# Attention of a vision transformer layer: weighted values and their sums as four streams of 256 queries, four tiles of exponentials, and matrix pieces run whole or in quarters

## The chip, the cores and the metric

One core of one Trainium2 chip runs the whole kernel as one program. The metric is the device time of one execution in microseconds (us); "the median" is the median over several executions. TensorE is the matrix engine (PE in the profile; its weight loads are listed apart as PEld), VectorE is DVE, ScalarE is ACT, GpSimd is POOL, and SyncE (SP) issues the transfers.

## The reference

Sixteen images of 512x512 are cut into 1,024 patches each and embedded into 256 channels. One transformer layer follows: attention with 8 heads of 32 channels, where every key is first sent through a sum of 256 sines and 256 cosines, and then a network with a shared branch and four experts of which two are weighed in. Cut to what matters here:

```python
h = patches(x) @ W.T + b
qkv = layernorm(h) @ w_qkv
q, k, v = to_heads(split(qkv))
k = sum(a[f] * sin(f * k) + b[f] * cos(f * k) for f in 1..256)
attn = softmax(q @ k.T / sqrt(32))
h = h + (attn @ v) @ w_out + b_out
h = h + shared(layernorm(h)) + sum(top2 weights * experts(layernorm(h)))
```

The softmax is not shifted by its maximum here: the kernel computes exponentials, the weighted sum of the values, and the sum of the exponentials, and divides at the end. All of it is fp32.

## The kernel before

The plain path (`plain_path`) builds the whole instruction stream for the 16 images in Python, with an order that a planner decides while building. The planner keeps an estimated clock for each engine.

*The two kinds of work.* Work with a **fixed order** makes up rounds. There are 128 attention steps (16 images, 4 pairs of heads, 2 halves of 512 queries) and 512 groups of key transforms, so each round has four groups and one attention step, which belongs to the groups of two rounds earlier:

- a group (`load_waves`, `turn_waves`, `sine`, `mix`, `times_fast`): two tiles w and one tile f are turned on POOL, go through the sine on ScalarE (`sine`, L972, after a table load at the first of a round), are mixed on TensorE in eight tiles of 64x32 (`mix`, L996, written kan) and multiplied on VectorE (`times_fast`, L1010, "prod"). `add_up` (L1029, written red) sums products over two groups.
- an attention step: eight tiles of scores (`score`, L1094, written sT, two matmuls of 512 columns), their exponentials (`exponential`, L1109, written es), eight weighings (`weigh`, L1126, written av), and `normalize` (L1152 to L1171) on VectorE. `ATTENTION` gives the order on TensorE: s is a score with its exponential, w a weighing, r a sum of products: "ssssrwwsswwsswwww". So four scores come first, then weighings and scores in pairs, and after the eighth score four more weighings.

On ScalarE each round is: one table load for the sine, twelve sines, one table load for the exponential (L1240), eight exponentials.

**Pieces** are the rest, generators in four chains: `tokens` (tok, the patch embedding, 6 matmuls of 256 columns), `keys` (k), `queries` (q), `values` (v), `project` (proj), `gates`, and `networks` (s1p, s2p, e1p, e2p, wb, e3p). Where a generator says `yield GO` it wants TensorE next. `run` decides each time whether the fixed head or a piece goes: a piece may go when it is ready clearly before the fixed work (by `IDLE`, or, when the fixed head has the same tiling as the array now, by two `SWITCH`), or when it is due. `retile` counts a change of tiling at `SWITCH`, 0.18 us, in the planner's clock.

*Tilings.* Most pieces, scores and transposes use the whole array of 128x128. Weighings, sums of products, gates and the experts' second layer use four column tiles of 128x32 side by side (`TILINGS`), and the mixing uses 64x32.

*Buffers that matter.* Two big PSUM buffers are shared in turn by kan and sT, so a score waits until the product or the exponential two places earlier has read its buffer (`big_deps`). The exponentials have three tiles (`esp`): an exponential waits for the weighing three places earlier. One PSUM bank holds the accumulator of the weighings (`avp`): the next step's first weighing waits for `normalize`. Two `side` banks serve the pieces.

*Weighing before.* The 512 columns of the accumulator are 512 queries. Its 128 rows are, in four blocks of 32: the values of head 0, the sums of head 0, the sums of head 1, the values of head 1. The tile v has 96 columns for each pair: values, ones, values. So four matmuls of 512 columns run side by side, two of them against ones:

```python
for i in range(4):
    nc.tensor.matmul(
        out=acc[0][ts(i, HD), :],
        lhsT=v[:, kc, p % NPAIR, ds(HD * (i - i // 2), HD)],
        rhs=es[:, ts(i // 2, 512)], ...
```

`normalize` takes reciprocals of the whole accumulator in two halves of 256 columns, multiplies 32x512 for each head, and adds up a check over 128x512.

Of the kernel before, what the change touches and what calls it, by code (L numbers as in the profile page):

```python
# [18 lines left out]
P = 128  # L19
E = 256  # L20
NPAIR = 4
HD = 32
# [25 lines left out]
NW = 8  # L48
GS = 4
NW5 = 4 * (NE + 1)  # L50
PE, ACT, DVE, POOL, SP = "pe", "act", "dve", "pool", "sp"
GO = PE, None
# [6 lines left out]
TILINGS = {"mix": (64, 32), "av": (128, 32), "red": (128, 32)}  # L59
ATTENTION = "ssssrwwsswwsswwww"  # L60

@with_exitstack
def plain_path(ctx: ExitStack, tc: tile.TileContext, a: dict, out: bass.AP, verdict: bass.AP):
# [29 lines left out]
    esp = pool("esp", 3)  # L93
# [107 lines left out]
    v = const.tile([P, NT, NPAIR, 96], FP, tag="v", name="v")  # L201
    nc.gpsimd.memset(v[:, :, :, 32:64], 1.0)
# [43 lines left out]

    def together(at, queue):
# [18 lines left out]
    def matmul(out, lhsT, rhs, start, stop):  # L266
        now["stream"] += max(rhs.shape[-1], P)
        nc.tensor.matmul(out=out, lhsT=lhsT, rhs=rhs, start=start, stop=stop)  # L268
# [23 lines left out]
    def step(c):  # L292
# [6 lines left out]
        on = need[0] if isinstance(need, tuple) and need[0] in clock else None  # L299
        if on:  # L300
# [40 lines left out]
    def wanting(engine):  # L341

        for c, ch in enumerate(chains):
# [3 lines left out]
            if len(need) > 2 and now["table"] != need[2]:  # L347
                continue
# [53 lines left out]

    def run():

        while True:
# [8 lines left out]
                or (at < fixed[0] - 2 * SWITCH if follows else at < then - IDLE)  # L414
                or (not follows and chains[c]["due"] > 0 and at <= then)
# [64 lines left out]
    def tokens(b, half):  # L480
# [5 lines left out]
        for t in range(4):  # L486
            j = 4 * half + t
            yield "x", b, j
            yield GO
# [28 lines left out]
    def keys(b, rows, blks=(0, 1)):  # L518
# [7 lines left out]
        for blk in blks:  # L526
            yield "hnT", b, blk
            yield GO
# [44 lines left out]
    def queries(b, rows):  # L573
# [7 lines left out]
        for blk in range(2):  # L581
            yield GO
# [14 lines left out]
    def values(b):  # L597
# [5 lines left out]
        for t0 in range(0, NT, 2):  # L603
            yield GO
# [12 lines left out]
            for s in range(2):  # L617
                nc.scalar.copy(
                    v[:, ds(t0, 2), 0 : NPAIR - 1, ds(64 * s, HD)],
# [5 lines left out]
    def last_values(b):  # L625
# [3 lines left out]
        for s in range(2):  # L629
            nc.gpsimd.tensor_copy(  # L630
                v[:, :, NPAIR - 1, ds(64 * s, HD)], images[b]["last"][:, :, s, :]
# [61 lines left out]
    def project(b, half):  # L693
# [3 lines left out]
        for pr in range(2):  # L697
            yield GO
# [19 lines left out]
    def gates(b, half, late=False):  # L718
# [9 lines left out]
        yield GO  # L728
# [11 lines left out]
        now["piece"] = TILINGS["red"]  # L740
# [18 lines left out]
    def networks(b, half, late=False):  # L759
# [25 lines left out]
        def first_of_expert(e):  # L785
            yield GO
# [6 lines left out]
        def second_of_experts(u, e1):  # L793
            yield GO
            ps = side_tile("e2p")
            now["piece"] = TILINGS["av"]
# [25 lines left out]
        for m in range(2):  # L822
            yield GO
# [4 lines left out]
        yield GO  # L828
# [276 lines left out]
    def exponential(att, kc):  # L1105
# [6 lines left out]
        old = att * NT + kc - 3  # L1112
# [4 lines left out]
    def weigh(att, kc):  # L1117
# [3 lines left out]
        def action():  # L1121
# [3 lines left out]
            for i in range(4):  # L1125
                nc.tensor.matmul(  # L1126
                    out=acc[0][ts(i, HD), :],
                    lhsT=v[:, kc, p % NPAIR, ds(HD * (i - i // 2), HD)],
                    rhs=es[:, ts(i // 2, 512)],
                    start=(kc == 0),  # L1130
                    stop=(kc == NT - 1),
                )
# [9 lines left out]
    def normalize(att):  # L1142
# [4 lines left out]
        def reciprocal(half):  # L1147
            def action():
                if half == 0:
                    rc[0] = kup.tile([P, 512], FP, tag="rc", name="rc")  # L1150
# [24 lines left out]
        for half in range(2):  # L1175
            reciprocal(half)
# [826 lines left out]
```

## Time and profile before

| | |
|---|---|
| median of 3 executions | 4131.01 us (4130.44 to 4134.47) |
| the profiled execution's own time | 4124.1 us |
| its span on the core | 4122.6 us, mean granted TensorE clock 0.994 |
| share of 16 transfer engines' time | 80.2% for the main queue |
| weighing av, TensorE | 8192 matmul records, 956.9 us busy, mean 596 ns |
| score sT, TensorE | 2048 records, 691.5 us, mean 449 ns |
| mixing kan, TensorE | 8192 records, 635.0 us, mean 600 ns |
| exponential es, ScalarE | 1024, 1035.8 us, mean 1023 ns |
| sine w and f, ScalarE | 1024 and 512, 1020.7 and 513.6 us, mean 1048 ns |
| reciprocal rc, VectorE | 256 of 128x256, 431.8 us, mean 1727 ns |
| division aT, VectorE | 256 of 32x512, 176.1 us, mean 688 ns |
| check rc, VectorE | 128 of 128x512, 87.1 us, mean 680 ns |
| one image (eight rounds) in the middle | 248 us, from a last score to that of eight steps later |

An fp32 matmul has two records (two passes over its columns); the scores are in a format with one pass. Matmuls overlap, so a record's mean length is longer than what it adds to the time: what counts is the distance from one start to the next. Busy times are unions of the records and hold some waiting. The record of an engine that waits shows the idle time in front of it and who ended it.

### The profile page before, as it was taken

The page shows a single profiled execution, that of the slowest core. Times are in us where ns is not written, and L with a number is a line of the kernel's source. Part 1 is how long each engine was busy: PE and PEld are TensorE (multiplying, and loading weights), DVE is VectorE, ACT ScalarE, POOL GpSimd, SP SyncE. Part 2 cuts the span into 40 slices and gives each one's busy share as a digit, 9 for nine tenths or more (in the row PEclk, how much of TensorE's full clock was granted, in tenths as well). Part 3 has the DMA queues.
Part 4 walks back from the last instruction along what each step waited for, and adds up shares of the span by engine and source line. Part 5 has one row for each costly group of instructions (what it writes and reads, how often), then busy time and mean ns, then how long its engine had stood idle before and what let it go on. Part 6 is the DMA issues. An engine that isn't in the chain of part 4 may idle for free.

```text
span 4122.6 us, 76263 instructions
## 1 busy us (share of the span) xinstructions
PE 3972.3 (96%) x27105; PEld 1756.1 (43%) x27105; DVE 2818.9 (68%) x4172; ACT 3283.9 (80%) x3939; POOL 3195.2 (78%) x2328
## 2 busy tenths in 40 slices
PE   7889999999999999999999999999999999999998
PEld 4324344444444444444444444444444444443334
DVE  4666767777667776767767667776767767668652
ACT  2688888888888878888788888878888788888873
POOL 3988878787787887878787787887878788787750
PEclk9999999999999999999999999999999999999999
DMA  7998878878878888888888878888888878878850
GB/s 219 262 246 220 245 206 225 247 220 226 236 213 244 233 233 220 225 241 225 244 221 225 235 215 241 234 232 220 225 241 223 247 217 225 236 204 235 211 144 17
DMA packets 587512, 914.82 MB, mean 222 GB/s; under 512 B 58828, under 2 KB 177524, under 8 KB 587124
## 3 DMA queue, kind: packets, MB, share of 16 engines
q1 hardware_dynamic: 580880, 906.98, 80.2%
q8 instruction: 218, 3.57, 0.4%
q10 hardware_dynamic: 6244, 2.88, 0.3%
q14 instruction: 170, 1.39, 0.1%
HBM read 758.64 MB, written 150.99 MB: 221 GB/s over the span
## 4 chain that ended last, share of the span: by engine, by line
PE 60%; ACT 16%; DMA 8%; DVE 6%; issue 5%; SPq 3%; POOL 1%; ACTq 0%; DVEq 0%; POOLq 0%
PE av L1126 14%; PE sT L1094 10%; ACT w L972 7%; PE kan L996 6%; PE tok L268 5%; PE red L1029 5%; PE e1p L268 4%; DMA w<-ud 4%; ACT f L972 3%; PE proj L268 3%; SPq L926 2%; PE k L268 2%; PE q L268 2%; DVE f L1010 2%; PE s1p L268 2%
## 5 line engine op out<-in xcount | busy, mean ns | idle before, releaser
L962 POOL TENSOR_TENSOR w<-w,lane 128x1024 int32<-128x1024 int32 x1024 | 1924.9, 1895 | 535.4 <-DMA w<-ud 300.0
L1109 ACT ACTIVATE es<-sT 128x1024 f32<-128x1024 f32 x1024 | 1035.8, 1023 | 531.0 <-PE av L1126 303.3
L962 POOL TENSOR_TENSOR f<-f,lane 128x1024 int32<-128x1024 int32 x512 | 970.1, 1895 | 145.1 <-DVE f L947 127.6
L972 ACT ACTIVATE w<-w 128x1024 f32<-128x1024 int32 x1024 | 1020.7, 1048 | 36.9 <-POOL w L962 25.0
L1126 PE MATMUL av<-es,v 128*32 128x512 f32 x8192 | 956.9, 596 | 2.2 <-DVE rc L1171 2.2
L1152 DVE RECIPROCAL rc<-av 128x256 f32<-128x256 f32 x256 | 431.8, 1727 | 544.1 <-PE av L1126 544.1
L1094 PE MATMUL sT<-q,k 128*128 128x512 f32 x2048 | 691.5, 449 | 44.9 <-DVE f L1010 27.0
L1010 DVE TENSOR_TENSOR f<-kan,f 128x1024 f32<-128x1024 f32 x512 | 604.3, 1218 | 142.2 <-ACT f L972 112.6
L996 PE MATMUL kan<-w,coef 64*32 64x512 f32 x8192 | 635.0, 600 | 47.4 <-ACT w L972 46.4
L947 DVE STREAM_SHUFFLE f<-src 128x1024 int32<-128x1024 int32 x512 | 674.6, 1360 | 0.5
L1094 PEld LDWEIGHTS sT<-q,k 128*128 128x128 f32 x2048 | 348.5, 189 | 422.1 <-issue 178.5
L972 ACT ACTIVATE f<-f 128x1024 f32<-128x1024 int32 x512 | 513.6, 1048 | 2.8 <-POOL f L962 2.8
L1126 PEld LDWEIGHTS av<-es,v 128*32 128x32 f32 x8192 | 239.7, 109 | 552.9 <-issue 493.0
L268 PE MATMUL tok<-wt,x 128*128 128x256 f32 x1536 | 363.3, 388 | 17.0 <-DMA x<-in_xT 13.1
L268 PEld LDWEIGHTS tok<-wt,x 128*128 128x128 f32 x1536 | 291.3, 193 | 98.8 <-issue 37.1
L996 PEld LDWEIGHTS kan<-w,coef 64*32 64x32 f32 x8192 | 135.0, 105 | 420.4 <-ACT w L972 266.9
L1029 PE MATMUL red<-f,pack 128*32 128x512 f32 x2048 | 273.6, 604 | 1.5 <-DVE f L1010 1.3
L268 PE MATMUL e1p<-hT,w1e 128*128 128x512 f32 x480 | 234.2, 610 | 0.8 <-ACT s L826 0.4
L972 ACT ACT_TABLE_LOAD x128 | 164.2, 1283 | 22.2 <-DMA w<-ud 19.9
L1159 DVE TENSOR_TENSOR aT<-av,rc 32x512 f32<-32x512 f32 x256 | 176.1, 688 | 6.7
L467 ACT ACTIVATE hn<-h,less,rstd 128x256 f32<-128x256 f32 x256 | 144.1, 593 | 37.8 <-POOL less L459 37.8
L1240 ACT ACT_TABLE_LOAD x128 | 164.2, 1283 | 2.3
(129 smaller groups left out, 3726.4 us busy)
## 6 DMA issues: line engine op xcount, KB each, us to landing
w<-ud SPq DMA_DIRECT2D x2048, 256.0 KB
q<-qd SPq DMA_DIRECT2D x512, 128.0 KB
k<-kd SPq DMA_DIRECT2D x128, 512.0 KB
x<-in_xT SPq DMA_DIRECT2D x128, 384.0 KB
ud<-u SPq DMA_DIRECT2D x64, 512.0 KB
ud<-ui SPq DMA_DIRECT2D x64, 512.0 KB
src<-ud SPq DMA_DIRECT2D x512, 64.0 KB
qd<-qhi SPq DMA_DIRECT2D x64, 256.0 KB
```

The costliest lines, as they stand in the source:

```text
L268: nc.tensor.matmul(out=out, lhsT=lhsT, rhs=rhs, start=start, stop=stop)
L947: nc.vector.stream_shuffle(w, sources[g // 8].rearrange("p r n -> p (r n)"), [4 * (g % 8) + i // 8 for i in range(32)],)
L962: nc.gpsimd.tensor_tensor(w, w, f.to_broadcast([P, N]), ALU.mult)
L972: nc.scalar.activation(x, w, AF.Sin, scale=TURN * 2.0**-32)
L996: nc.tensor.matmul(out=ps[ds(64 * j + 32 * blk, 32), ts(r, 512)], lhsT=coef[ts(r, 64)].rearrange("p e f j -> p (e f j)"), rhs=w[ts(r, 64), ...
L1010: nc.vector.tensor_mul(w, kan.pop(g), w)
L1029: nc.tensor.matmul(out=rows_of_pair[p][ts(2 * i + r, 32), :], lhsT=pack[:, ds(PACK0 - 16 * (k % 2) - 2 * (k // 2), 32)], rhs=prod[:, ts(r, ...
L1094: nc.tensor.matmul(out=ps[:, ts(s, 512)], lhsT=k4[:, 2 * s + kc // 4, ts(kc % 4, P)], rhs=q4[:, s, :], start=True, stop=True,)
L1109: nc.scalar.activation(es, scores.pop(kc), AF.Exp, scale=SCALE)
L1126: nc.tensor.matmul(out=acc[0][ts(i, HD), :], lhsT=v[:, kc, p % NPAIR, ds(HD * (i - i // 2), HD)], rhs=es[:, ts(i // 2, 512)], start=(kc == 0),
L1152: nc.vector.reciprocal(rc[0][:, part], acc[0][:, part])
L1159: nc.vector.tensor_mul(aT[ds(64 * (i % 2) + HD * s, HD), i // 2, ts(qb, 512)], acc[0][ds(96 * s, HD), :], rc[0][ds(HD + HD * s, HD), :],)
```

## The change

- The weighing becomes eight matmuls of 256 columns. The four column tiles are now head 0 and head 1 of the first 256 queries, then head 0 and head 1 of the second 256. The first four matmuls put the weighted values into columns 0 to 255, the other four the sums into columns 256 to 511 of the same rows, against a tile of ones of its own (`ones32`). The ones leave v, which has 64 columns for each pair.
- `normalize` takes one reciprocal of 128x256, divides 64 rows by 256 columns twice, and its check covers 128x256.
- The exponentials have four tiles in place of three (`NES`), so each waits for the weighing four places earlier.
- `GO` now says "whole". Pieces that say `ANY` are whole matmuls when the array is whole, and quarters when it is in column tiles: each matmul is then issued as four of 32 output rows. After kan, `tiling_of` looks at the next three fixed entries. Of the pieces tok, k, q, v, proj, s1p, e1p and s2p are of this kind. The gates and the experts' second layer, which were in column tiles before, say "columns"; transposes, wb and e3p stay whole.
- In `run`, the stricter rule against a piece that would break a tiling is applied only when the piece would have another tiling (`apart`). `ATTENTION` and the due times are as before.

```diff
-GO = PE, None
+NES = 4
+GO = PE, None, "whole"
+ANY = PE, None, "either"
+COLUMNS = (128, 32)
...
-    esp = pool("esp", 3)
+    esp = pool("esp", NES)
...
-    v = const.tile([P, NT, NPAIR, 96], FP, tag="v", name="v")
-    nc.gpsimd.memset(v[:, :, :, 32:64], 1.0)
+    v = const.tile([P, NT, NPAIR, 2 * HD], FP, tag="v", name="v")
+    ones32 = const.tile([P, HD], FP, tag="ones32", name="ones32")
+    nc.gpsimd.memset(ones32, 1.0)
...
+    def tiling_of(kind):
+        if kind == "columns":
+            return COLUMNS
+        if kind == "whole":
+            return None
+        if now["tiling"] in (None, COLUMNS):
+            return now["tiling"]
+        ahead = [TILINGS.get(key[0]) for _, _, key, _ in queues[PE]["fixed"][:3]]
+        return COLUMNS if COLUMNS in ahead and None not in ahead[: ahead.index(COLUMNS)] else None
...
     def matmul(out, lhsT, rhs, start, stop):
         now["stream"] += max(rhs.shape[-1], P)
-        nc.tensor.matmul(out=out, lhsT=lhsT, rhs=rhs, start=start, stop=stop)
+        if now["piece"] != COLUMNS:
+            nc.tensor.matmul(out=out, lhsT=lhsT, rhs=rhs, start=start, stop=stop)
+            return
+        for i in range(4):
+            nc.tensor.matmul(
+                out=out[ts(i, 32)], lhsT=lhsT[:, ts(i, 32)], rhs=rhs, start=start, stop=stop
+            )
...
+    def apart(c):
+        return tiling_of(chains[c]["need"][2]) != now["tiling"]
...
-                or (at < fixed[0] - 2 * SWITCH if follows else at < then - IDLE)
-                or (not follows and chains[c]["due"] > 0 and at <= then)
+                or (at < fixed[0] - 2 * SWITCH if follows and apart(c) else at < then - IDLE)
+                or (not (follows and apart(c)) and chains[c]["due"] > 0 and at <= then)
...
-            yield GO
+            yield ANY
             ps = side_tile("tok")[:, 0:E]
...
-        old = att * NT + kc - 3
+        old = att * NT + kc - NES
         if old >= 0:
             deps.append(("av", *divmod(old, NT)))
...
-            for i in range(4):
-                nc.tensor.matmul(
-                    out=acc[0][ts(i, HD), :],
-                    lhsT=v[:, kc, p % NPAIR, ds(HD * (i - i // 2), HD)],
-                    rhs=es[:, ts(i // 2, 512)],
-                    start=(kc == 0),
-                    stop=(kc == NT - 1),
-                )
+            for half in range(2):
+                for i in range(4):
+                    nc.tensor.matmul(
+                        out=acc[0][ts(i, HD), ts(half, 256)],
+                        lhsT=ones32 if half else v[:, kc, p % NPAIR, ts(i % 2, HD)],
+                        rhs=es[:, ds(512 * (i % 2) + 256 * (i // 2), 256)],
+                        start=(kc == 0 and half == 0),
+                        stop=(kc == NT - 1),
+                        skip_group_check=True,
+                    )
...
-                nc.vector.reciprocal(rc[0][:, part], acc[0][:, part])
+            nc.vector.reciprocal(rc[0], acc[0][:, 256:512])
...
-                    aT[ds(64 * (i % 2) + HD * s, HD), i // 2, ts(qb, 512)],
-                    acc[0][ds(96 * s, HD), :],
-                    rc[0][ds(HD + HD * s, HD), :],
-                )
+                    aT[ds(64 * (i % 2), 2 * HD), i // 2, ds(512 * qb + 256 * half, 256)],
+                    acc[0][rows, 0:256],
+                    rc[0][rows, :],
+                )
```

## The prediction

> **What bounds the kernel now.** I read the page's engine shares first, then the chain of waits in one stretch of the middle, then the waits of all engines, then the timeline of two engines at the end of an attention step.
>
> ```profile
> PE 3972.3 (96%) x27105; PEld 1756.1 (43%) x27105; DVE 2818.9 (68%) x4172; ACT 3283.9 (80%) x3939; POOL 3195.2 (78%) x2328
> ```
>
> TensorE is busy 96% of the span; no other engine is above 80%. A busy TensorE is not yet a streaming one, so the next view, the chain of waits (start, length, what), tells what each piece costs after each neighbour.
>
> ```profile
> 2020.51 1.88 PE kan L996 x32
> 2022.38 1.00 PE red L1029 x8
> 2023.38 1.91 PE e1p L268 x4
> 2025.30 0.93 PE sT L1094 x4
> 2026.22 1.72 PE q L268 x4
> 2027.94 0.93 PE sT L1094 x4
> 2028.87 0.99 PE red L1029 x8
> 2029.87 1.72 PE av L1126 x16
> 2031.58 1.92 PE s2p L268 x4
> ...
> 2034.42 1.85 PE av L1126 x16
> ```
>
> The same work has two prices. A two-chunk piece of 512 columns is 1.72 us after whole-array work (q) and 1.91 to 1.92 after 32-column work (e1p after red, s2p after av). A pair of weighings is 1.72 after red, which has their tiling, and 1.85 after a score. So a change of tiling costs about 0.195 us into the whole array and 0.13 into column tiles. By the same subtraction over the middle of the trace: 0.165 from whole to the 64x32 tiles of kan (1.88 against 1.72), 0.195 from kan to whole, 0.135 from kan to columns (0.99 for a red of 0.858), 0.15 to 0.16 from columns to kan. Nothing else separates the pieces: TensorE is bound by streaming plus changes of tiling, and by some waits:
>
> ```profile
> ACT es L1109 <- PE av L1126: 303.3, 348, 4.0
> ACT es L1109 <- PE sT L1094: 225.1, 267, 8.9
> PE kan L996 <- ACT w L972: 46.4, 59, 4.8
> PE sT L1094 <- DVE f L1010: 27.0, 61, 1.0
> ```
>
> TensorE waits for ScalarE's sines, and for big PSUM buffers that the products and exponentials free. ScalarE waits much longer for TensorE: 303 us of that is an exponential that wants one of three tiles back from a weighing.
>
> ```profile
> 2037.63 1.50 PE L1094 MATMUL sT<-q,k 128*128 128x512 f32 x4
> 2038.81 1.02 ACT L1109 ACTIVATE es<-sT 128x1024 f32<-128x1024 f32 x1
> 2039.06 3.64 PE L1126 MATMUL av<-es,v 128*32 128x512 f32 x32
> 2040.25 1.02 ACT L1109 ACTIVATE es<-sT 128x1024 f32<-128x1024 f32 x1 [0.42 <-PE av L1126]
> 2041.29 1.28 ACT L972 ACT_TABLE_LOAD   x1
> 2042.59 1.06 ACT L972 ACTIVATE w<-w 128x1024 f32<-128x1024 int32 x1
> ```
>
> These are the last two scores of a step (7th and 8th), their exponentials, the four weighings, and the start of the next round's sines. The eighth exponential starts 0.42 us after the seventh is done, because it waits for the fifth weighing. From here to the next step's exponentials ScalarE has table load, twelve sines, table load; in this stretch ScalarE and not TensorE is short of time.
>
> [...] The trace has a pass of 512 columns fp32 at 0.429 us (1.72 for four), and one of 256 columns at 0.2158 (12 tok passes in 2.59). [...]
>
> **The change part by part.** The sum is against the profiled execution (4124.1 us, span 4122.6); the median of the runs, 4131.0, lies 6.9 above it and gets the same difference.
>
> 1. *Weighing as 8 matmuls of 256 columns in place of 4 of 512.* Four column tiles run together, so a step was 2 x 0.429 = 0.858 and becomes 4 x 0.2158 = 0.863: 1,024 steps x 0.005 = +5 us. Twice as many matmuls and weight loads: a weight load of 32 columns takes 110 ns (row of L1126), less than a pass of 0.216, and gate, which streams only 128 columns through four column tiles, does its 16 records in 0.44 us behind a weighing, at 0.109 per pass. So weight loads hide.
>
> 2. *Pieces in quarters.* A whole piece of 512 columns and four quarters side by side stream equally long (1.72 for q, 1.72 for two weighings). What goes is changes of tiling. I counted them in the two orders of TensorE's instructions:
>
>    Whole to columns 474 before and 409 after; columns to whole 558 and 461; whole to kan 279 and 132; kan to whole 195 and 80; kan to columns 118 and 245; columns to kan 34 and 193.
>
>    At the prices above (0.155 for the last) this is 275.7 us before and 243.5 after. With part 1, streaming and changes of tiling together come to 3824.6 us before and 3797.7 after: **-26.9 us**. 1,176 matmuls of tok, k, q, v, proj, s1p, s2p, e1p become quarters.
>
> 3. *Where the pieces now lie.* Because a quarter piece no longer breaks the tiling, the rule lets it between two weighings. TensorE's work from the fourth to the eighth score of a step grows from 7.51 to 8.19 us, and its work from the eighth score to the fourth of the next step falls from 20.89 to 19.99 (means over 121 middle rounds). In that second stretch ScalarE needs 18.77 us from the start of the eighth exponential to the end of the next step's second, which the fourth score waits for (18.86 after), at the pitches of the trace: sine 0.946, exponential 0.915, table load 1.29, hidden layers 0.57, normalizing 0.49. So the pieces move out of the stretch in which ScalarE is late, 0.9 us per round.
>
> 4. *Four tiles of exponentials.* With three, the eighth exponential waits for the fifth weighing; with four for the fourth, which is done before the eighth score. From the end of the eighth score's streaming to the start of its exponential the trace has 1.62 us on the mean (median 1.29). By the same instructions at the same prices it comes to 1.67 before; after, the seventh exponential or the eighth score sets it, 0.73. ScalarE starts its stretch 0.94 us sooner: about what part 3 takes.
>
>    I summed parts 3 and 4 round by round. For each landmark (kan of the four groups, each score of the next step, its weighings) I took ScalarE's or VectorE's work up to it less TensorE's work up to it, both from the eighth score, and of these the largest if above nothing. Before: 124.9 us in 121 rounds. The trace, as time between eighth scores less streaming and changes of tiling, has 174.1, with a correlation of 0.94 over the rounds and 1.20 x sum + 0.20 us per round as the fit. After: 107.4, by the fit 153.2: **-20.9 us**. With three tiles in the new order the sum would be 197.1, by the fit 260.5: +86. So this is the small difference of two large terms and the least certain one.
>
> 5. *Normalizing.* Two reciprocals (1.727 each), two divisions (0.688) and the check (0.680) become one reciprocal, two divisions of 64x256 and a check of 128x256. The nearest row for these is h<-tok, 128x256, 0.406. Per step 5.5 us becomes 3.0, some 320 us of VectorE in all. In the middle it is hidden: the next weighing comes 20 us later. Two steps at the end are bare: the timeline has a weighing at 4039.41 that waits 2.17 for the check, and projections behind the last division. **-4 us.** Less VectorE work ahead of the products could give a few us more, or nothing; I take nothing.
>
> 6. *Rest.* A smaller memset of v at the start, gates' and experts' second layer with their tiling named: nothing, same instructions.
>
> Sum: -26.9 - 20.9 - 4 = -51.8, so 4072 for the profiled execution and **4079** for the median.
>
> **The rivals.**
>
> *Rival 1, slower: ScalarE's start isn't earlier.* Place: the eighth exponential. If it still starts 1.3 us or more behind its score (the seventh being late, or pieces before the eighth score), part 4 falls away and part 3 stays: +86 - 26.9 - 4 = +55, 4186. Between -51.8 at a mean start of 0.73 us and +55 at 1.67, in proportion, it turns slower by over 0.2% from 1.26 us on. For it: 303 us of such waits are there, and the pieces do move into the weighings. Against: in the lines above the seventh exponential was done 0.42 before.
>
> *Rival 2, slower: TensorE can't take the instructions so fast.* 27,105 matmul records become about 42,350, in runs of 54 ns each where it streams 256 columns (22,300 of them). The trace of before shows that rate only in bursts (kan: 32 records in 1.72 us); over 64 records its best is 78 ns. [...]
>
> *Rival 3, no change: the waits eat the gain.* For it: the middle of a small difference is soft, and the rounds of after are less alike. If the waits grow by what the changes of tiling save, 4131 - 27 + 27 - 4 = 4127. Against: the fit holds with a correlation of 0.94.
>
> *Rival 4, faster still.* Products come sooner on a freer VectorE, and half of the 153 us of waits goes too: 4131 - 27 - (174 - 77) - 4 = 4003. For it: 27 us of waits of scores for products. Against: those products wait for sines themselves.
>
> **How the numbers follow.** Forecast (4050 to 4115): 0.62. Rival 4 and what lies below 4050: 0.08. Rival 3, within 0.2% (8 us, about what a measurement of this kernel tells from no change): 0.12. Rival 1: 0.12. Rival 2: 0.06. Faster 0.70, same 0.12, slower 0.18. The range takes in the no-change case and half of rival 4's room: 4045 to 4142 leaves out rivals 1 and 2 and the lowest values.
>
> **What would show it.** In the chain: a quarter piece after av or kan at 1.72 and 1.85 in place of 1.91; a pair of weighings at 1.73 after red; gaps of 0.2158 per pass. In the timeline: the eighth exponential right behind the seventh. Among the waits: es <- av far below 303 us; kan <- w and sT <- es no larger than now. VectorE's busy time near 2,500 us. Wrong would be: av steps above 0.87 us (rival 2), kan and sT waits that grow (rival 1).

## The result, and the profile after

| | before | after |
|---|---|---|
| median of 4 executions | 4130.73 us | 4085.28 us (4081.02 to 4097.31) |
| ratio, 95% interval | 1 | 0.9893 (0.9871 to 0.9915) |
| the profiled execution's own time | 4124.1 us | 4081.02 us |
| its span | 4122.6 us | 4079.5 us |
| matmul records | 27,105 | 42,353 |

The changed kernel is faster by 45 us, 1.1%, in the medians, and by 43.1 us in the spans of the two profiled executions. The forecast was 4079 us. A single execution can lie several us to either side: 23 of the kernel before ran from 4125.4 us (mean granted clock 0.994) to 4142.5 (0.990). The page's engine shares of the changed kernel come first:

```profile
PE 3925.2 (96%) x42353; PEld 1889.6 (46%) x42353; DVE 2538.8 (62%) x4044; ACT 3252.8 (80%) x3939; POOL 3196.3 (78%) x2328
```

TensorE is again busy for 96% of the span, now with 56% more records. VectorE gave up 280 us of work. The chain of waits in the middle of the changed kernel's trace (start, length, what):

```profile
2002.16 1.02 PE kan L1020 x16
2003.18 1.85 PE e1p L287 x16
2005.03 1.02 PE kan L1020 x16
2006.05 1.00 PE red L1053 x8
2007.05 1.32 PE sT L1118 x4
...
2010.54 0.99 PE red L1053 x8
2011.53 1.73 PE av L1151 x32
2013.26 0.44 PE wb L284
2013.69 0.92 PE sT L1118 x4
2014.62 1.86 PE av L1151 x32
...
2028.78 1.88 PE kan L1020 x32
2030.66 1.86 PE v L287 x32
2032.52 2.77 PE kan L1020 x32
2035.29 1.00 PE red L1053 x8
2036.29 1.73 PE v L287 x32
```

Here kan is the mixing, red a sum of products, sT a score and av a weighing; L287 is a piece in quarters, L284 a whole one. A quarter piece of v behind red, which has its tiling, is 1.73 us, where a whole e1p in that place was 1.91. Behind kan it is 1.85 or 1.86. A pair of weighings is now 32 records, and still 1.73 behind red and 1.86 behind a score. So in these lines streaming cost nothing more, and a quarter piece meets the array as a weighing does. The kan at 2032.52 shows what is left: 2.77 us for the 32 records that take 1.88 at 2028.78 in the same trace, so some 0.9 us of it is a wait.

The waits of the changed kernel (engine, line, for whom; total, times, longest):

```profile
DVE rc L1175 <- PE av L1151: 611.0, 114, 9.8
ACT es L1133 <- PE sT L1118: 479.7, 310, 8.6
...
PE kan L1020 <- ACT w L996: 44.6, 54, 3.7
PE sT L1118 <- ACT es L1133: 21.3, 47, 1.2
PE sT L1118 <- DVE f L1034: 16.3, 28, 2.7
...
PE sT L1118 <- DMA k<-kd: 8.9, 6, 2.7
```

One line of the kernel before belongs beside them:

```profile
PE sT L1094 <- ACT es L1109: 12.0, 35, 0.8
```

The 303.3 us in which an exponential waited for a weighing are gone; the exponentials now wait for their scores alone. But TensorE's own waits hardly moved: kan for sines went from 46.4 to 44.6 us, scores for products from 27.0 to 16.3, and scores for exponentials rose from 12.0 to 21.3, which the prediction had named as a sign of being wrong. In six places a score now waits for the transfer of its keys, 8.9 us in all; the kernel before has no such wait, and the same order in experiments 1, 2 and 4 has 1.3 to 1.7 us of it. The wait that vanished was ScalarE's, and the sums below show how little of it reached the time.

The timeline of TensorE and ScalarE over the end of an attention step of the changed kernel:

```profile
2047.43 1.21 PE L1118 MATMUL sT<-q,k 128*128 128x512 f32 x4
2048.27 1.94 ACT L1133 ACTIVATE es<-sT 128x1024 f32<-128x1024 f32 x2 [1.06 <-PE sT L1118]
...
2049.02 0.61 PE L1151 MATMUL av<-es,ones 128*32 128x256 f32 x8
...
2049.89 0.61 PE L1151 MATMUL av<-es,ones 128*32 128x256 f32 x8
...
2050.22 1.28 ACT L996 ACT_TABLE_LOAD   x1
...
2050.75 0.61 PE L1151 MATMUL av<-es,ones 128*32 128x256 f32 x8
```

The four matmuls are the seventh and eighth scores. Their exponentials are one stretch of 1.94 us with nothing between them, and the table load follows 0.01 us behind. Before, 0.42 us lay between the two.

I split the difference of 43.1 us in the spans by the prediction's own terms. "List" is streaming plus changes of tiling at the prediction's prices, over the whole program. "Waits" is the time between eighth scores in 121 middle rounds less the list's part of it; it is what is left over, and not idle time alone. "Lateness" is the prediction's sum over these rounds, computed from each kernel's order of instructions and not from its time. The last column but one is the mean distance in the middle rounds from the end of the eighth score's streaming to its exponential.

| | list | waits | lateness | eighth exponential behind | span |
|---|---|---|---|---|---|
| before | 3824.6 us | 174.1 us | 124.9 us | 1.61 us | 4122.6 us |
| after | 3797.7 us | 171.7 us | 107.4 us | 0.76 us | 4079.5 us |

The list gives -26.9, the waits -2.4, the stretch ahead of the middle rounds -4.3 beyond the list's part and the stretch behind them -9.3 (from 115.6 us in all to 106.3, with 88 us of list in both): -42.9 together. So in these two traces the gain is the changes of tiling, the end and the start. The waits, from which the prediction had expected 20.9 us, gave next to nothing. TensorE's idle time by the pages, span less busy time, didn't fall either: 150.3 us before and 154.3 after. Each of these figures is from one execution, so a difference of a few us among the waits, between these two or any two programs below, is not to be relied on.

### The profile page after: what moved, and what is told of

The parts are those of the page before. It is cut to its first block, busy times and chain, and to the rows that moved or that the text cites. A ratio compares the mean times of both kernels' runs of the same rounds, so it can differ in the third digit from the quotient of the medians.

```text
span 4079.5 us, 106618 instructions
## 1 busy us (share of the span) xinstructions
PE 3925.2 (96%) x42353; PEld 1889.6 (46%) x42353; DVE 2538.8 (62%) x4044; ACT 3252.8 (80%) x3939; POOL 3196.3 (78%) x2328
## 4 chain that ended last, share of the span: by engine, by line
PE 59%; ACT 16%; DMA 11%; DVE 5%; issue 4%; SPq 2%; POOL 2%; ACTq 0%; DVEq 0%; POOLq 0%
PE av L1151 14%; PE sT L1118 10%; ACT w L996 7%; PE kan L1020 6%; DMA w<-ud 6%; PE e3p L284 4%; PE red L1053 4%; PE tok L284 4%; ACT f L996 3%; PE e1p L287 2%; DVE f L1034 2%; ACT es L1133 2%; PE tok L287 2%; SPq L950 2%; PE e1p L284 2%
## 5 line engine op out<-in xcount | busy, mean ns | idle before, releaser
L1133 ACT ACTIVATE es<-sT 128x1024 f32<-128x1024 f32 x1024 | 1006.0, 1022 | 481.1 <-PE sT L1118 479.7
L1118 PE MATMUL sT<-q,k 128*128 128x512 f32 x2048 | 668.8, 439 | 52.1 <-ACT es L1133 21.3
L1020 PE MATMUL kan<-w,coef 64*32 64x512 f32 x8192 | 612.7, 600 | 44.9 <-ACT w L996 44.6
L1151 PE MATMUL av<-es,v 128*32 128x256 f32 x8192 | 637.7, 383 | 1.2 <-ACT es L1133 1.2
L1151 PE MATMUL av<-es,ones 128*32 128x256 f32 x8192 | 631.0, 380 | 0.0
L1175 DVE RECIPROCAL rc<-av 128x256 f32<-128x256 f32 x128 | 224.9, 1757 | 611.0 <-PE av L1151 611.0
L1151 PEld LDWEIGHTS av<-es,ones 128*32 128x32 f32 x8192 | 266.7, 110 | 177.2 <-issue 2.1
L284 PE MATMUL tok<-wt,x 128*128 128x256 f32 x792 | 185.0, 385 | 13.3 <-DMA w1s<-in_sW 13.1
L287 PE MATMUL tok<-wt,x 128*32 128x256 f32 x2976 | 172.2, 379 | 3.2 <-DVE ui L579 3.2
L284 PEld LDWEIGHTS tok<-wt,x 128*128 128x128 f32 x792 | 152.0, 193 | 38.1 <-issue 13.5
```

Source lines behind the costliest of these rows:

```text
L287: nc.tensor.matmul(out=out[ts(i, 32)], lhsT=lhsT[:, ts(i, 32)], rhs=rhs, start=start, stop=stop)
L1020: nc.tensor.matmul(out=ps[ds(64 * j + 32 * blk, 32), ts(r, 512)], lhsT=coef[ts(r, 64)].rearrange("p e f j -> p (e f j)"), rhs=w[ts(r, 64), ...
L1118: nc.tensor.matmul(out=ps[:, ts(s, 512)], lhsT=k4[:, 2 * s + kc // 4, ts(kc % 4, P)], rhs=q4[:, s, :], start=True, stop=True,)
L1133: nc.scalar.activation(es, scores.pop(kc), AF.Exp, scale=SCALE)
L1151: nc.tensor.matmul(out=acc[0][ts(i, HD), ts(half, 256)], lhsT=ones32 if half else v[:, kc, p % NPAIR, ts(i % 2, HD)], rhs=es[:, ds(512 * ( ...
L1175: nc.vector.reciprocal(rc[0], acc[0][:, 256:512])
```

## The experiments

Each has its median and its ratio to the kernel before with a 95% interval, both from runs on one chip. That kernel's median was between 4130.5 and 4138.1 from one group of runs to another, so ratios are what is compared across groups. Where a difference of medians across groups is given, the one by ratios stands beside it, in us of a kernel before of 4131; the spans and the waits are those of one profiled execution each.

**1. Whole pieces in the changed kernel's order.** On the changed kernel; the order and every wait stay, and the pieces are whole matmuls wherever they stand.

```diff
-        if now["piece"] != COLUMNS:
+        if True:
```

> The changed kernel with its order of instructions untouched, but every piece issued as whole matmuls. Theory A (changes of tiling cost what the chain shows): changes of tiling rise from 1520 to 1743 in the plain path, and streaming plus changes from 3797.7 to 3844.6 us, +47; the waits stay or fall a little, since TensorE has more to do where ScalarE is late (round sums 107 to 99). So 30 to 47 us above the changed kernel, about 4125. Rival B (quarters gain nothing, the gain lies in the fourth tile and VectorE): within 10 us of the changed kernel.

4129.5 us, ratio 0.9989 (0.9982 to 0.9996): slower than the changed kernel by 44 us in the medians and by 40 in the ratios. The list says +47 (3844.6 against 3797.7, with 1743 changes of tiling in place of 1520). The waits come out the same, 171.7. So in this order quarters are worth, within some 10 us, what counting changes of tiling says. Note where it ends, though: the new order without quarters is as slow as the old one.

**2. Three tiles of exponentials in the changed kernel's order.**

```diff
-    esp = pool("esp", NES)
+    esp = pool("esp", 3)
```

> The changed kernel with its order untouched and three tiles of exponentials in place of four. Theory A: the eighth exponential waits for the fifth weighing again, its start behind the eighth score goes from 0.76 to about 1.7 us on the mean, and the round sums from 107 to 197 us; +86 to +110, about 4180 to 4195, slower than the kernel before. Rival C (ScalarE has slack there, the fourth tile only moves idle time): within 15 us of the changed kernel.

4198.31 us, ratio 1.0155 (1.0135 to 1.0176), 113 us slower than the changed kernel in the medians and 108 in the ratios, a little above the range expected. The list is the same, the waits are 287.2 in place of 171.7, the eighth exponential stands 1.77 us behind its score. The waits of this kernel:

```profile
ACT es L1133 <- PE av L1151: 417.2, 360, 4.6
ACT es L1133 <- PE sT L1118: 237.6, 264, 8.2
```

The wait for the weighing is back, larger than in the kernel before. This is the place of the prediction's first rival, and about its size (+55 us to the kernel before; the ratio says +64). With pieces between its weighings, this order is slower than the kernel before if it has no fourth tile.

**3. Four tiles in the order of before.** The weighing stays four matmuls of 512 columns; v loses its ones to make room.

```diff
-    esp = pool("esp", 3)
+    esp = pool("esp", 4)
...
-    v = const.tile([P, NT, NPAIR, 96], FP, tag="v", name="v")
+    v = const.tile([P, NT, NPAIR, 2 * HD], FP, tag="v", name="v")
+    ones32 = const.tile([P, HD], FP, tag="ones32", name="ones32")
...
-                    lhsT=v[:, kc, p % NPAIR, ds(HD * (i - i // 2), HD)],
+                    lhsT=ones32 if i in (1, 2) else v[:, kc, p % NPAIR, ts(i // 2, HD)],
```

> The kernel before, its order untouched, with a fourth tile of exponentials (the ones come out of v to make room, as in the change, but weighing and normalizing are as before). Theory A: start of the eighth exponential 0.73 us behind its score in place of 1.61, round sums from 125 to 84 us, by the fit of the prediction -49: about 4082, as much as the whole change. Rival C: within 15 us of the kernel before.

4101.94 us, ratio 0.9927 (0.9910 to 0.9943), which is 30 us. The span fell by 22.6 us, the waits by 19.6; the fit of the prediction had promised 49 for a lateness that falls from 124.9 to 84.1. A hint of what held the rest back stands in the shares of the chain that ended last. The kernel before, then this one:

```profile
PE 60%; ACT 16%; DMA 8%; DVE 6%; issue 5%; SPq 3%; POOL 1%; ACTq 0%; DVEq 0%; POOLq 0%
```

```profile
PE 66%; DVE 10%; ACT 10%; DMA 7%; issue 3%; SPq 2%; POOL 2%; ACTq 0%; DVEq 0%; POOLq 0%
```

ScalarE's share of the chain falls from 16 to 10%, as it should when its stretch starts sooner, and VectorE's rises from 6 to 10%. My reading was that ScalarE's lateness had covered VectorE's. The prediction had taken nothing for VectorE's relief, so the next four runs are on that reading.

**4. The short normalizing undone in the changed kernel.** The reciprocal and the two divisions run twice.

```diff
+            for _ in range(2):
                 nc.vector.reciprocal(rc[0], acc[0][:, 256:512])
...
+                for _ in range(2):
                     nc.vector.tensor_mul(
```

> The changed kernel, order untouched, with the reciprocal and both divisions issued twice, which gives VectorE back about 2.5 us per attention step (some 320 us). Theory A: bare only at the two last steps, +4 us, at most +10. Rival D (the freer VectorE is where the gain comes from: products and with them scores and mixings sooner): +25 or more.

4211.04 us, ratio 1.0195 (1.0178 to 1.0212): 126 us slower in the medians, 125 in the ratios. Its engine shares, the shares of the chain (the changed kernel's, then its own) and four of its waits:

```profile
PE 3938.2 (94%) x42353; PEld 1896.9 (45%) x42353; DVE 2862.8 (68%) x4428; ACT 3263.2 (78%) x3939; POOL 3196.9 (76%) x2328
```

```profile
PE 59%; ACT 16%; DMA 11%; DVE 5%; issue 4%; SPq 2%; POOL 2%; ACTq 0%; DVEq 0%; POOLq 0%
PE 53%; ACT 14%; DVE 12%; DMA 12%; issue 5%; SPq 3%; POOL 1%; ACTq 0%; DVEq 0%; POOLq 0%
```

```profile
PE kan L1020 <- ACT w L996: 93.4, 67, 4.1
PE e3p L284 <- DVE e L841: 24.9, 18, 2.9
...
PE sT L1118 <- DVE f L1034: 22.1, 40, 1.4
PE kan L1020 <- ACT hnT L502: 13.4, 6, 2.2
```

VectorE has 324 us more to do, about as much as in the kernel before, and is still busy for only 68% of the span. Yet it takes 12% of the chain in place of 5%. The waits are 294.0 in place of 171.7, with list and lateness unchanged. TensorE's busy time rose by 13 us and its idle time by 117, so the lower granted clock of this run (mean 0.985 against 0.993) isn't what made most of the difference. The largest of TensorE's waits is for sines, which VectorE doesn't compute: so some of the delay must have gone around through other engines before it arrived.

**5 and 6. Half the normalizing in the kernel before, and in experiment 3.** Both kernels leave 256 queries of each step undivided, and the memset of aT stands in for them. The check, too, covers 256 columns. In experiment 6 the same edit stands on experiment 3.

```diff
+    nc.gpsimd.memset(aT, 0.0)
...
+                if half == 0:
                     nc.vector.reciprocal(rc[0][:, part], acc[0][:, part])
...
-                    acc[0][ds(96 * s, HD), :],
-                    rc[0][ds(HD + HD * s, HD), :],
+                    acc[0][ds(96 * s, HD), 0:256],
+                    rc[0][ds(HD + HD * s, HD), 0:256],
```

> The kernel before, order untouched, with normalizing cut to the length that it has in the change: one reciprocal of 256 columns, both divisions and the check over 256 columns (the other 256 queries of each step are left undivided). Theory A (VectorE hidden in the middle, bare at the end): -4 us, at most -10. Theory E (VectorE is a second queue, of which the doubled reciprocals showed the edge, but with three tiles ScalarE's late start comes last): -5 to -20. Theory D (the freer VectorE is a main part of the gain by itself): -30 or more.

> The same cut of normalizing in the kernel before with four tiles of exponentials, order untouched (again 256 queries of each step undivided). The fourth tile alone gave 4102. Theory A: another -4 us, 4098. Theory E: now normalizing comes last, so -20 to -35 more, 4067 to 4082, which is at or below the whole change without one quarter piece. Theory D: the same step as in the run with three tiles, -30 or more.

With three tiles: 4125.6 us, ratio 0.9984 (0.9974 to 0.9994), a gain of 5 us by the medians (4130.51 beside it) and 7 by the ratio. With four tiles: 4083.63 us, ratio 0.9895 (0.9878 to 0.9911). Against experiment 3 the ratio fell by 0.0032, 13 us, and the span by 18.1; but the mean granted clock of this trace was 0.996 and that of experiment 3's 0.994, and 0.002 of a list of 3824.6 us is 8 us, an estimate of what the clock alone can have given. The chain's shares went back:

```profile
PE 68%; ACT 12%; DMA 7%; DVE 5%; issue 3%; SPq 2%; POOL 1%; ACTq 0%; DVEq 0%; POOLq 0%
```

So by the middle of the ratios the same relief of VectorE gave 7 us while ScalarE was late and 13 once it was less so, but the intervals leave room for no difference at all. The traces lean to the reading. VectorE's share of the chain, 10% with four tiles, became 5%, where with three tiles it was 6% before and after. TensorE's idle time, span less busy time, went from 143.0 to 130.7 us with four tiles and from 150.3 to 150.4 with three. The engine shares of experiments 5, 3 and 6, in turn, whose spans are 4124.5, 4100.0 and 4081.9 us:

```profile
PE 3974.1 (96%) x27105; PEld 1757.6 (43%) x27105; DVE 2518.3 (61%) x4044; ACT 3285.0 (80%) x3939; POOL 3198.7 (78%) x2329
PE 3957.0 (97%) x27105; PEld 1754.5 (43%) x27105; DVE 2821.5 (69%) x4172; ACT 3256.3 (79%) x3939; POOL 3195.8 (78%) x2328
PE 3951.2 (97%) x27105; PEld 1753.5 (43%) x27105; DVE 2524.9 (62%) x4044; ACT 3256.2 (80%) x3939; POOL 3195.2 (78%) x2329
```

With one trace each, this supports the reading and doesn't show it. And a second reading: in the order of before, four tiles and half the normalizing alone reach 0.9895, where the whole change reaches 0.9893. Between this kernel and the changed one lie the new order, the weighing by 256 columns and the quarters. Experiment 1 has the first two without the quarters, and there the list is 20.0 us longer and the waits 30.8 (171.7 against 140.9), 47 us by the spans. The quarters take 47 of the list off again.

**7. The planned cost of normalizing doubled too.** On experiment 4, so that the order knows of the longer work.

```diff
-            put(DVE, "norm", 0.4, deps, ("divide", att, half), action)
+            put(DVE, "norm", 0.8, deps, ("divide", att, half), action)
...
-        put(DVE, "norm", 1.67, [("av", att, NT - 1)], ("reciprocal", att), reciprocal)
+        put(DVE, "norm", 3.34, [("av", att, NT - 1)], ("reciprocal", att), reciprocal)
```

> The changed kernel with the reciprocal and the divisions issued twice and their planned costs doubled too, so that the planner lays the order with them. Theory E: the 123 us of the doubled run came from work that the order had not counted on in front of the products; planned, most of it goes, and the time lies 20 to 60 us above the changed kernel, 4105 to 4145. If VectorE's load itself is the limit: within 30 us of the doubled run, 4180 or more.

4224.98 us, ratio 1.0229 (1.0212 to 1.0246): a miss, 80 us above the upper end of what I had expected, and in the range that was to mean that VectorE's load itself is the limit. The order that came out has a lateness of 198.6 in place of 107.4, so it differs from experiment 4 in more than where VectorE's work was planned. It tells neither whether planning for the work helps nor whether the load is the limit.

**8. Whole pieces, and an order planned for them.**

```diff
-ANY = PE, None, "either"
+ANY = PE, None, "whole"
```

> The changed kernel without quarters: every piece that could be either is whole, and the planner lays the order knowing it. Changes of tiling 1595 in the plain path, streaming and changes 3818.8 us, +21 against the change. The round sums of ScalarE's lateness are 172 us (107 in the change), by the fit +70. Theory A: about 4150 to 4175. If the waits don't follow these sums and only changes of tiling count: 4106.

4165.39 us, ratio 1.0090 (1.0074 to 1.0107), as the lateness of its order (172.3) had said: list 3818.8, waits 229.4. With four tiles and the short normalizing it is slower than the kernel before. That made the order itself the suspect.

**9 and 10. All parts of the change, in the order of before.** The planner is told of three tiles, whole pieces and the old normalizing, while the work is that of the changed kernel; quarters are taken wherever the array is in column tiles (42,809 and 42,689 records of matmuls, against 42,353). In the second, the planner also counts ScalarE and VectorE as starting 0.27 us behind TensorE's end and not 0.06; in the trace of before, where TensorE ended the wait, the reciprocal starts 0.25 us behind the end of a weighing's streaming and an exponential 0.26 behind that of its score (medians).

```diff
-            now["piece"] = tiling_of(need[2])
+            now["quarters"] = need[2] == "either" and tiling_of(need[2]) == COLUMNS
+            now["piece"] = COLUMNS if need[2] == "columns" else None
...
-        old = att * NT + kc - NES
+        old = att * NT + kc - 3
```

```diff
-        return max([clock[engine]] + [done[d] + LAG for d in deps])
+        return max([clock[engine]] + [done[d] + (0.27 if d[0] in ("av","score","mix","red") and engine != PE else LAG) for d in deps])
```

> The new weighing, the short normalizing, four tiles and quarters, but laid in exactly the order of the kernel before: the planner counts pieces as whole, normalizing at its old cost and three tiles, and keeps the old rule; a piece becomes quarters only where the array happens to be in column tiles. Changes of tiling 1620 in the plain path, streaming and changes 3814.1 us (before 3824.6, the changed kernel 3797.7), round sums of ScalarE's lateness 86 us. Theory F (the parts are worth what the single runs showed, and the new order gave back about what quarters save): 10 us below the run with four tiles and short normalizing, 4073, below the changed kernel. If the new order is itself worth something: at or above the changed kernel, 4085 or more.

> The same, with one number of the planner set nearer the trace: other engines see the end of a weighing, score, mixing or sum 0.27 us after TensorE's streaming (0.06 before; the trace has 0.25 to 0.29). This changes the order a little. Streaming and changes 3815.3 us, round sums 80 us. Theory F: within 10 us of the run above, rather below, 4060 to 4080.

4084.24 us, ratio 0.9876 (0.9857 to 0.9894), and 4080.77, ratio 0.9868 (0.9849 to 0.9887). The first differs from experiment 6 by the quarters, by the weighing of 256 columns and by dividing all queries; its list is 10.5 us shorter, its waits 12.3 longer, the medians are equal and the ratios 8 us apart with intervals that overlap. So what quarters are worth in the old order isn't settled. Neither kernel is apart from the changed one.

**11. Two planned costs 4% dearer.** On the changed kernel; the work is the same, only its order changes, and with it how many pieces run in quarters (40,733 records of matmuls against 42,353).

```diff
-        put(ACT, "fixed", 0.96 + change, [("turn", g, j)], ("sine", g, j), action)
+        put(ACT, "fixed", 1.0 + change, [("turn", g, j)], ("sine", g, j), action)
...
-        put(ACT, "fixed", 0.99, deps, ("exp", att, kc), action)
+        put(ACT, "fixed", 1.03, deps, ("exp", att, kc), action)
```

> The changed kernel, all instructions the same in number and kind, with the sine planned at 1.00 us in place of 0.96 and the exponential at 1.03 in place of 0.99; only the order changes. Streaming and changes 3800.4 us, +3 against the change, round sums of ScalarE's lateness 172 us against 107. Theory G (the order that the planner happens to lay is as large a term as any part of the change): +60 to +100, 4145 to 4185, slower than the kernel before. If orders by this planner are much alike: within 20 us of the changed kernel.

4192.44 us, ratio 1.0131 (1.0111 to 1.0152). The list is 3800.4, the waits 277.2, the lateness 172.0. A change of a few hundredths of a microsecond in what the planner believes made the same work slower by 107 us in the medians and 98 in the ratios.

**12. An order picked by its sum.** I laid out 64 orders of the changed kernel's work with other planner constants. By my sums their list ran from 3798 to 3825 us, their lateness from 48 to 221. The one with the least of both together is experiment 10 with one more edit:

```diff
-LAG, LANDS, TABLE, PER_COLUMN, SWITCH, IDLE = 0.06, 2.0, 1.28, 1.0 / 600, 0.18, 0.3
+LAG, LANDS, TABLE, PER_COLUMN, SWITCH, IDLE = 0.06, 2.0, 1.28, 1.0 / 600, 0.16, 0.3
```

> As the run with the lag known, but a change of tiling planned at 0.16 us in place of 0.18, which lays another order. It is the one of 64 orders of the same instructions (other lags, idle bounds, paces and planned costs of a change of tiling, on the changed kernel and on the order of before) with the least streaming plus waiting by the sums: streaming and changes of tiling 3823.0 us, +8 against the run with the lag known, round sums of ScalarE's lateness 48 us against 80. Theory G (the order decides, and these sums tell it): -8 to -32 against that run, 4048 to 4073, the fastest of all. If the sums don't carry over to a picked order: 4080 to 4110.

4071.86 us (4070.53 to 4078.18), ratio 0.9854 (0.9838 to 0.9871), with a lateness of 48.3 and waits of 137.8. Two of TensorE's waits for ScalarE:

```profile
PE sT L1121 <- ACT es L1136: 35.3, 78, 0.8
PE kan L1023 <- ACT w L999: 24.6, 24, 5.4
```

The wait of kan for sines is 24.6 us, from 44.6 in the changed kernel; that of scores for exponentials rose to 35.3, from 21.3. This kernel has the lowest median of all that ran, and its list is 25 us longer than the changed kernel's. It is faster than the kernel before beyond doubt; from the changed kernel it stands 13 us off in the medians and 16 in the ratios, with intervals that touch at 0.9871. From experiment 10 it isn't apart: the ratios differ by 0.0014, and where the lateness fell by 31 us the waits fell by 9 and the list grew by 8. So whether the sums pick the best of near orders stays open.

The measures of all programs, in us, beside those of the first table:

| | list | waits | lateness | eighth exponential behind | span |
|---|---|---|---|---|---|
| 1 whole pieces, same order | 3844.6 | 171.7 | 98.9 | 0.76 | 4129.1 |
| 2 three tiles, same order | 3797.7 | 287.2 | 197.1 | 1.77 | 4198.7 |
| 3 before, four tiles | 3824.6 | 154.5 | 84.1 | 0.76 | 4100.0 |
| 4 normalizing doubled | 3797.7 | 294.0 | 107.4 | 0.80 | 4209.6 |
| 5 before, half normalizing | 3824.6 | 181.5 | 124.9 | 1.61 | 4124.5 |
| 6 the same, four tiles | 3824.6 | 140.9 | 84.1 | 0.75 | 4081.9 |
| 7 doubled and planned | 3799.9 | 308.7 | 198.6 | 0.73 | 4229.9 |
| 8 whole pieces, own order | 3818.8 | 229.4 | 172.3 | 0.84 | 4163.7 |
| 9 all parts, order of before | 3814.1 | 153.2 | 86.4 | 0.75 | 4081.0 |
| 10 the same, lag known | 3815.3 | 146.7 | 79.6 | 0.74 | 4078.4 |
| 11 planned 4% dearer | 3800.4 | 277.2 | 172.0 | 0.82 | 4192.3 |
| 12 picked by its sum | 3823.0 | 137.8 | 48.3 | 0.97 | 4076.6 |

Over the 14 programs the measured waits go with the lateness at a correlation of 0.83. Without the two whose normalizing is doubled it is 0.95, and the fit is 1.08 times the lateness plus 61 us. Single programs lie up to 30 us from this line (experiment 11 above it, the kernel before 22 below), so it tells a bad order from a good one, and not 20 us between two.

## Why the prediction was right, by its steps

The prediction gives two ranges, 4050 to 4115 and 4045 to 4142 us; 4085 lies in both, and the forecast of -51.8 us lies inside the measured interval. The parts don't all fit. The list is a count, and experiment 1 supports it; but the waits gave 18.5 us less than forecast, and start and end gave 13.6 us where 4 were counted. That the second error made up for half of the first is luck.

**Step 1, the weighing by 256 columns: right.** Weighings start 0.86 to 0.87 us apart (0.863 predicted): the halves against ones in the timeline above, at 2049.02, 2049.89 and 2050.75.

**Step 2, quarters: right.** -26.9 was the count, and experiment 1 supports the count's basis: 47 by list, 44 by medians, 40 by ratios, waits unchanged.

**Steps 3 and 4, pieces into the weighings and the fourth tile: right in mechanism, wrong in size.** The eighth exponential was to stand 0.73 us behind its score and stands 0.76. With three tiles in the new order the waits were to be 86 us above those of the kernel before, and were 113 above (287.2). But the pair was to give -20.9 and gave -2.4. The term that was mis-sized is the fit's remainder: the part of the waits that the lateness doesn't contain. It was 174.1 - 124.9 = 49 before; by the fit it was to be 153.2 - 107.4 = 46 after, and it was 171.7 - 107.4 = 64. This took back nearly all of the 17.5 us by which the lateness did fall. The prediction had called this the least certain term; it had no reason why the remainder should grow. The 8.9 us in which scores wait for keys are new in this remainder; what the rest is, no run isolates. The fit had been made over the rounds of one program and was carried to another order, where single programs turned out to lie up to 30 us off.

**Step 5, normalizing: wrong in the middle, about right at the end.** "In the middle it is hidden" holds for the kernel before: half the normalizing saved 5 to 7 us there (experiment 5), of which the trace has 3.4 behind the middle rounds (115.6 to 112.2). It fails for the changed kernel, where taking the saving away costs 126 (experiment 4). Something had covered VectorE's work before and didn't after. That it was ScalarE's lateness, which the fourth tile removes, is the reading to which experiments 3, 5 and 6 lean for the old order, where they give 13 us by the ratios. It doesn't account for the 126: in the changed kernel the lateness is 107.4, above the 84.1 of those experiments, and ScalarE's share of the chain is 16% again. So the new order, or the work laid into it without being planned for, must count for most of it; which of these, no run separates. In the result the relief doesn't stand out: the waits are 294.0 us with the normalizing doubled and 171.7 without, where the prediction had 153.2 with no credit for it. The argument in the prediction was that the next weighing comes 20 us later. That is true of the weighing (20.0 us on the mean in the kernel before, 18.4 in the changed one, from the start of a step's last to that of the next step's first); the products were named, and nothing was taken for them without a reason. By which of them the delay travels (products, the key transforms, the hidden layers) no run isolates; that TensorE's wait for sines doubled in experiment 4 shows that it isn't one step. At the end, the stretch behind the middle rounds shrank by 9.3 us, but normalizing is only a part of that: doubling it in the changed kernel gives back 3.5 (106.3 to 109.8), and halving it took 3.4 in experiment 5 and 5.2 in experiment 6 (115.1 to 109.9). So the -4 was about right. With all parts in the order of before this stretch is 110.2, so the other 4 or so go with the new order.

**Step 6: the start.** -4.3 us ahead of the middle rounds, where nothing was taken. No run isolates it. Over all programs this stretch, less its list, runs from 91.8 to 96.5 us without a pattern (96.3 before, 92.0 after), so it may be chance.

**The rivals.** Rival 1 (ScalarE's start isn't earlier) has its mechanism confirmed and its condition refuted, by experiment 2 and by 0.76 us. Rival 2 (TensorE can't take the instructions) is refuted by the changed kernel's trace: 53.4 ns a record over 128 in a row (last section), and weighings 0.86 to 0.87 us apart. What a slower rate would have cost was the author's estimate, which no run shows. Rival 3 (waits eat the gain) came half true: they ate what the waits themselves were to give, not the list's gain. Rival 4 (a freer VectorE takes half the waits) named an engine that matters, as experiment 4 shows; scores waited less for products (27.0 to 16.3 us), and the sum of the waits shows nothing of it.

**What wasn't in the prediction: the order is a term of its own.** The changed kernel's work takes 4072 to 4192 us by its order, and by the quarters that go with the order (experiments 12 and 11), and the whole change is worth 45. In the order of before, the fourth tile with half the normalizing already reaches the changed kernel's time; the new order with its weighing costs 47 us (the spans of experiments 6 and 1), and the quarters pay that back. The prediction's sums took the order in through the lateness, without naming it as a part of the change.

## What to carry to other kernels

Work that is hidden in one order needn't be hidden in another: normalizing twice as long cost the changed kernel 126 us, and half of it saved the kernel before 5 to 7. So cost "hidden" work again in the kernel that comes out. Where a planner lays the order, price the order that comes out and not the edit, and try a few neighbouring orders before judging an edit by its time. A wait that vanishes from a page (303 us here) isn't time gained by itself: 20 to 30 us came of it in the old order, and 2 in the change.

## What was not expected of the hardware

TensorE takes a weight load and a matmul each 53.4 ns over 128 records in a row, 53.7 over 200 and 67.7 over 500, in the changed kernel's trace; the best of the kernel before over 64 was 78. That is as fast as four column tiles stream 256 columns (0.2158 us for four), so no cost of the 15,248 additional records, in quarters and weighings, beyond the list is seen: without the 7,056 of the quarters the waits are the same (experiment 1), and a pair of weighings is 1.73 us. The longer program's instructions took 337 packets on their queue (q8 of the page) in place of 218. The new forms on VectorE, three groups of the changed kernel (what, times; busy, mean ns of one; idle before):

```profile
L1175 DVE RECIPROCAL rc<-av 128x256 f32<-128x256 f32 x128 | 224.9, 1757 | 611.0 <-PE av L1151 611.0
L1180 DVE TENSOR_TENSOR aT<-av,rc 64x256 f32<-64x256 f32 x256 | 107.8, 421 | 5.9
L1192 DVE SCALAR_TENSOR_TENSOR rc<-rc,av 128x256 f32<-128x256 f32 x128 | 53.7, 420 | 3.6
```

64 rows by 256 columns take 421 ns where 32 rows by 512 took 688, and 128 rows take 420: here columns set the time and rows don't, as the nearest row (0.406) had let expect. The reciprocal of 128x256 takes 1757 ns, four times as long as the other two on as many columns. It is VectorE's dearest step in the normalizing, and the change halves its number.
